# Expert chunks of five row tiles in place of two, four and four, in a two-FFN macaron kernel

## The chip, the cores and the metric

The kernel runs on one core of one Trainium2 chip. The metric is device time in microseconds (us), lower is better. The engines are called as the profile calls them: PE is the matrix engine, PEld its weight loads, DVE the vector engine, ACT the scalar engine, POOL the GpSimd engine, SP the engine that issues plain DMAs.

## The reference

A macaron block on x of 4 x 2048 rows by 256: half a mixture-of-experts FFN, an attention step, half the same FFN again. Each FFN routes every row to two of eight experts; an expert takes at most 1280 rows (1.25 x 8192 / 8), highest weights first.

```python
x = x + 0.5 * ffn(layernorm(x))
x = x + attn(layernorm(x))
x = x + 0.5 * ffn(layernorm(x))

def ffn(x):                     # D = 256, F = 1024, E = 8, two experts per row
    probs = softmax(x @ router_w.T); topw, topi = top_k(probs, 2)
    ...                         # the first 1280 rows of each expert, by weight
    g = disp @ wg; u = disp @ wu               # 1280 x 256 by 256 x 1024, each expert
    eo = (silu(g) * u) @ wd                    # 1280 x 1024 by 1024 x 256
    out[rows] += eo * weight
```

All products are in fp32.

## The kernel before

Five stages follow each other: a first router, FFN one, attention (which ends with the logits of the second router), a second router, FFN two. Both FFNs are the function `experts`; only the rows' source and the target of its sums differ. The change lies in `experts` and in the class `RowList`, which it uses.

**An expert in chunks.** An expert's 1280 rows are ten tiles of 128 rows. `SIZES` cuts them into chunks of two, four and four tiles (`chunks`, lines 414 to 416), so that an FFN has 24 chunks. For each chunk the kernel gathers the rows by index (`gather`, one indirect DMA from POOL's queue for each tile), zeroes rows that the expert doesn't own (`blank`, on ACT), transposes them on PE (`turn`, one call for each half of D; `tr` is one PSUM bank, and ACT copies it to `xsT`), makes the hidden activations (`small_steps` or `large_steps`), and multiplies by wd (the down projection, lines 656 to 683): eight matmuls for each tile, an ACT scaling into `eo`, an indirect DMA from POOL that adds the rows to the target, and then `behind(k, i)`, which hangs other work behind tile `i`.

**The small chunk.** Two tiles are 256 columns. `small_steps` makes gate and up products plainly: over four steps `p`, 2 halves of F x 2 (gate, up) x 2 halves of D, 32 matmuls of 256 columns.

**The large chunk.** Four tiles are 512 columns. `large_steps` splits D, F and the columns in halves and uses the seven-product scheme of Strassen and Winograd: in each of four steps `p`, seven products for gate and seven for up, of BH = 256 columns each, so 56 matmuls in place of 64. Its operands are sums of weights (`ws`, made by `sums_of_w` on DVE once for each expert) and sums of inputs (`xs`, `sums_of_x`, once for each large chunk). The first product goes to the bank `one`, which ACT copies to `p1`; the others go to `mm`, three buffers of two banks. One buffer holds two products for gate and up, four matmuls in all. DVE reads them in adds of 1024 elements (512 where only one product is concerned) into `ct` and `uu`; ACT applies silu in place (L536), and DVE multiplies the halves into `h` (L451, through `finish`).

**The down projection's first two tiles** are ordered so that the products with the last step's `h` come last: twelve matmuls stand between the last up product and the first use of it.

**Row lists.** `RowList` turns slots into the list of an expert's row numbers: `high` makes three vectors of 1024 elements on DVE, `low(g)` a mask of 128 x 1024 for each of eight groups (L366, int16 operands and an fp16 result; the innermost axis of the mask is the slot, along which the row's own slot is a broadcast with step 0), `products(g)` eight small matmuls, `sum` and `end` bring the result back as indices. For expert 0 of an FFN nothing can start before its list is there (lines 632 to 640). For the next expert the masks are spread over `beside` (during the steps of the small chunk) and `behind` (during the down projections of the first two chunks), and the list ends in the second chunk.

**Order.** Inside `with tc.manual_schedule` (line 643) PE, DVE and ACT run in program order, so `beside(k, p)`, called after each step, and `behind(k, i)`, called after each tile of the down projection, set where the other work falls. POOL is ordered by the framework's scheduler, and so is everything on all engines for the first list of an FFN, which stands ahead of line 643.

Of the kernel before, what the change touches and what calls it, by code (L numbers as in the profile page):

```python
# [18 lines left out]
P = 128  # L19
# [7 lines left out]
def macaron_kernel(  # L27
# [31 lines left out]
    CH = 4  # L59
# [14 lines left out]
    JL = NJ // 4  # L74
    GT = T // (P // E)
# [28 lines left out]
    nc.gpsimd.iota(count, pattern=[[1, P]], base=0, channel_multiplier=0)  # L104

# [230 lines left out]
    TG = 8  # L336
    Q = P // 32
    HI = 32 // 2

    class RowList:  # L340
# [4 lines left out]
        def __init__(self, e, pool, ppool):  # L345
            self.e, self.pool, self.ppool = e, pool, ppool
            self.lo = {}

        def high(self):
            hi = self.pool.tile([P, T, HI], F16, tag="hi", name="hi", bufs=2)  # L350
            self.hv = self.pool.tile([P, T, 2, HI], F16, tag="hv", name="hv", bufs=2)
            shape = [P, T, HI]
            nc.vector.tensor_tensor(
                hi, spread(count[:, :HI].unsqueeze(1), shape),
                spread(slot_hi[:, self.e, :].unsqueeze(2), shape), ALU.is_equal,
            )
            nc.vector.tensor_scalar(self.hv[:, :, 0, :], hi, row_in, None, ALU.mult)
            nc.vector.tensor_tensor(self.hv[:, :, 1, :], hi, spread(row_of.unsqueeze(2), shape), ALU.mult)

        def begin(self):  # L360
            self.ps = self.ppool.tile([P, P], F32, tag="one", name="ix", bufs=1)

        def low(self, g):
            lo = self.pool.tile([P, TG, P], F16, tag="lo", name="lo", bufs=6)
            shape = [P, TG, P]
            nc.vector.tensor_tensor(  # L366
                lo, spread(count.unsqueeze(1), shape),
                spread(slot_lo[:, self.e, g * TG : (g + 1) * TG].unsqueeze(2), shape), ALU.is_equal,
            )
            self.lo[g] = lo  # L370

        def products(self, g):
            lo = self.lo.pop(g)
            for t in range(g * TG, (g + 1) * TG):
                q = slice(t % Q * 32, t % Q * 32 + 32)
                nc.tensor.matmul(  # L376
                    self.ps[q, :], self.hv[:, t, :, :].rearrange("p k i -> p (k i)"), lo[:, t % TG, :],
                    start=(t < Q), stop=(t >= T - Q),
                )
# [5 lines left out]
        def end(self):  # L385
            self.ps = self.ppool.tile([P, CH * P], F32, tag="tr", name="ixT", bufs=1)[:, :P]
# [20 lines left out]
    BH = CH * P // 2  # L407

    def experts(name, src, dst, wait_for, weights, wpool, pool, ppool):
# [3 lines left out]

        SIZES = [ST % CH] * (ST % CH > 0) + [CH] * (ST // CH)
        assert SIZES[0] < CH and len(SIZES) == 3
        chunks = [(e, sum(SIZES[:k]), n) for e in range(E) for k, n in enumerate(SIZES)]
        lists, got, xTs, ws, xs = {}, {}, {}, {}, {}
        sent = {-1: list(wait_for)}

        def gather(k):  # L420
            if k >= len(chunks):
                return
            e, i0, n = chunks[k]
            got[k] = []
            for i in range(i0, i0 + n):
                r = pool.tile([P, W], F32, tag="r", name="r", bufs=14)
                nc.gpsimd.indirect_dma_start(  # L427
                    out=r, out_offset=None, in_=src[:, :],
                    in_offset=bass.IndirectOffsetOnAxis(ap=lists[e][:, i : i + 1], axis=0),
                )  # L430
                got[k].append(r)

        def blank(k, *tiles):
            for i in tiles:
                if k < len(chunks) and i < chunks[k][2]:
                    e, r = chunks[k][0], got[k][i]
                    nc.scalar.mul(r[:, 0:D], r[:, 0:D], r[:, D + E + e : D + E + e + 1])

        def turn(k, c):
            if k >= len(chunks):  # L440
                return
            n = chunks[k][2]
            if c == 0:
                xTs[k] = pool.tile([P, DC, CH * P], F32, tag="xsT", name="xsT", bufs=2)
            ps = ppool.tile([P, CH * P], F32, tag="tr", name="tr", bufs=1)
            for i in range(n):
                nc.tensor.transpose(ps[:, i * P : (i + 1) * P], got[k][i][:, c * P : (c + 1) * P], ident)  # L447
            nc.scalar.copy(xTs[k][:, c, : n * P], ps[:, : n * P])  # L448
# [17 lines left out]
        def sums_of_x(k):  # L466
            if k >= len(chunks):
                return
            v = xTs[k]
            o = xs[k] = pool.tile([P, 4, BH], F32, tag="xs", name="xs", bufs=2)  # L470
# [6 lines left out]
        def banks():  # L477
            return ppool.tile([P, 2, CH * P], F32, tag="mm", name="mm", bufs=3)

        def small_steps(k):  # L480

            e, i0, n = chunks[k]
            xT, hs = xTs.pop(k), []
            for p in range(NF):
                ps = banks()
                for j in range(2):
                    fs = slice(p * P + j * FH, (p + 1) * P + j * FH)
                    for m in range(2):
                        for c in range(DC):
                            nc.tensor.matmul(  # L490
                                ps[:, j, m * BH : (m + 1) * BH], weights[e][m][:, c, fs], xT[:, c, :BH],
                                start=(c == 0), stop=(c == DC - 1),
                            )
                g = pool.tile([P, 2, BH], F32, tag="sg", name="sg", bufs=2)
                nc.scalar.activation(g, ps[:, :, :BH], AF.Silu)  # L495
                h = pool.tile([P, 2, CH * P], F32, tag="h", name="h", bufs=NF + 2)
                tt(h[:, :, :BH], g, ps[:, :, BH:], ALU.mult)
                hs.append(h)
                yield hs

        def large_steps(k):
            e, i0, n = chunks[k]
            xT, x4, hs = xTs.pop(k), xs.pop(k), []
            late = []

            def product(ps, p, j, c, b):

                for m in range(2):
                    if c is None:
                        a = ws[e][:, m, j, p * P : (p + 1) * P]  # L510
                    else:
                        a = weights[e][m][:, c, j * FH + p * P : j * FH + (p + 1) * P]
                    nc.tensor.matmul(ps[:, m * BH : (m + 1) * BH], a, b, start=True, stop=True)  # L513

            def finish(h, ct, qs):
                tt(h[:, qs, :], ct[:, qs, 0, :], ct[:, qs, 1, :], ALU.mult)
# [3 lines left out]
            def first_product(p):  # L520
                one = ppool.tile([P, CH * P], F32, tag="one", name="one", bufs=1)
                product(one, p, 0, 0, xT[:, 0, :BH])
                p1[p] = pool.tile([P, CH * P], F32, tag="p1", name="p1", bufs=2)
                nc.scalar.copy(p1[p], one)  # L524

            first_product(0)
            for p in range(NF):
                last = p == NF - 1

                ct = pool.tile([P, 5, 2, BH], F32, tag="ct", name="ct", bufs=2)  # L530
                blocks = ct.rearrange("p q m s -> p q (m s)")
                h = pool.tile([P, 2, CH * P], F32, tag="h", name="h", bufs=NF + 2)
# [4 lines left out]

                a = banks()
                product(a[:, 0, :], p, 0, 1, xT[:, 1, :BH])
                product(a[:, 1, :], p, 1, None, x4[:, 1, :])  # L540
                tt(blocks[:, 0:5:4, :], spread(p1.pop(p).unsqueeze(1), [P, 2, CH * P]), a, ALU.add)
                if late and not last:
                    finish(*late.pop())
                b = banks()
                product(b[:, 0, :], p, 0, None, x4[:, 0, :])
                product(b[:, 1, :], p, 2, None, x4[:, 2, :])
                uu = pool.tile([P, 2, CH * P], F32, tag="uu", name="uu", bufs=2)
                tt(uu, spread(blocks[:, 4:5, :], [P, 2, CH * P]), b, ALU.add)
                tt(blocks[:, 3, :], uu[:, 1, :], b[:, 0, :], ALU.add)
                if not last:  # L550
                    first_product(p + 1)
                d = banks()
                if not last:
                    product(d[:, 0, :], p, 3, None, xT[:, 1, BH:])
                    product(d[:, 1, :], p, 1, 1, x4[:, 3, :])
                    tt(blocks[:, 1:3, :], uu, d, ALU.add)
                    silu(slice(0, 4))
                    late.append((hq, ct, slice(0, 4)))
                else:

                    silu(slice(0, 4, 3))
                    product(d[:, 0, :], p, 1, 1, x4[:, 3, :])
                    tt(blocks[:, 2, :], uu[:, 1, :], d[:, 0, :], ALU.add)
                    silu(slice(2, 3))
                    finish(*late.pop())
                    d = banks()
                    product(d[:, 0, :], p, 3, None, xT[:, 1, BH:])
                    finish(hq, ct, slice(0, 4, 2))
                    tt(blocks[:, 1, :], uu[:, 0, :], d[:, 0, :], ALU.add)
                    silu(slice(1, 2))  # L570
                    finish(hq, ct, slice(1, 4, 2))
# [3 lines left out]
        EARLY = 5  # L575
# [579 lines left out]
```

## Time and profile before

| | |
|---|---|
| runs shown, us | 2085.96, 2082.26, 2086.65 (median 2085.96) |
| profiled execution, us | 2080.76 |
| its span, first to last instruction, us | 2078.9 |
| mean granted PE clock in it | 0.952 of full speed |
| FFN one: first matmul of the steps to last down matmul, us from the start | 126.69 to 935.70 |
| attention, first DMA, and second router's end | 940.29; 1238.18 |
| FFN two: first matmul of the steps to last down matmul | 1260.44 to 2069.19 |

The profile has one record for each instruction: the engine, the line, the operation, the tile written and the tiles read without buffer numbers, the shape. Start and duration are in us; in the table of groups the mean is in ns. A bracket behind a line gives the idle time ahead of the instruction and what ended it. An fp32 matmul leaves two records (the 160 row tiles of both FFNs have 8 down matmuls each, and line 663 has 2560 records), a transpose on PE leaves one.

### The profile page before, as it was taken

Reading aid. Unit: us, or ns where it says so; the run is one execution under the profiler, and the core shown is the slowest. Engines: PE = TensorE matmul, PEld = TensorE weight load, DVE = VectorE, ACT = ScalarE, POOL = GpSimd, SP = SyncE. Lnnn points to the kernel's source line nnn. Section 1 sums busy time; section 2 is a strip of 40 time slices with the busy share of each in tenths; the row PEclk is TensorE's granted clock in tenths of the full one; section 3 lists DMA queues with packets and bytes.
Section 4 is the critical chain, followed back from the end, with each engine's and each line's share of the span. In section 5 each row is a group of like instructions: output and inputs, shape, how many; then the busy total and the mean of one; then the engine's idle time right before and its main releaser. Section 6 shows DMA issues by size and latency. Waiting matters only on the chain.

```text
span 2078.9 us, 26374 instructions
## 1 busy us (share of the span) xinstructions
PE 1898.0 (91%) x10186; PEld 1635.5 (79%) x10186; DVE 1393.2 (67%) x2303; ACT 627.6 (30%) x1233; POOL 601.2 (29%) x640
## 2 busy tenths in 40 slices
PE   6369999999999999996999618999999999999998
PEld 4258888888888888885888416888888888888886
DVE  8867676767676767455789886767675766667554
ACT  5312222222222222224556402222222222323221
POOL 5323131313131313124556302313131314040411
PEclk8579999999999999998999858999999999999999
DMA  9911213122222211115012531222121313131201
GB/s 345 293 32 38 76 38 76 38 76 45 69 69 45 79 36 38 16 16 167 21 41 84 184 127 33 56 58 78 36 78 36 81 33 83 31 89 25 48 8 18
DMA packets 99916, 147.73 MB, mean 71 GB/s; under 512 B 7496, under 2 KB 86352, under 8 KB 99664
## 3 DMA queue, kind: packets, MB, share of 16 engines
q1 hardware_dynamic: 69056, 102.77, 14.5%
q0 software_dynamic: 30720, 43.27, 12.5%
q8 instruction: 81, 1.33, 0.3%
q14 instruction: 43, 0.35, 0.1%
q10 hardware_dynamic: 16, 0.01, 0.0%
HBM read 98.84 MB, written 55.57 MB: 74 GB/s over the span
## 4 chain that ended last, share of the span: by engine, by line
PE 82%; DVE 8%; issue 1%; POOL 1%; ACT 1%; DMA 1%; POOLq 0%; DVEq 0%; SPq 0%
PE mm L513 31%; PE mm L663 27%; PE mm L490 11%; PE one L513 5%; PE pc L842 2%; PE qp L785 2%; PE tr L447 2%; PE py L900 1%; DVE above L291 1%; DVE uu L451 1%; DVE lo L366 1%; PE ix L376 1%; DVE ct L451 1%; DVE q L796 0%; DVE st L912 0%
## 5 line engine op out<-in xcount | busy, mean ns | idle before, releaser
L663 PE MATMUL mm<-wdt,h 128*128 128x256 f32 x2560 | 572.6, 381 | 3.3 <-DVE ct L451 3.3
L663 PEld LDWEIGHTS mm<-wdt,h 128*128 128x128 f32 x2560 | 478.3, 190 | 75.0 <-PE tr L447 7.5
L513 PE MATMUL mm<-xs,ws 128*128 128x256 f32 x1536 | 352.4, 379 | 0.0
L513 PEld LDWEIGHTS mm<-xs,ws 128*128 128x128 f32 x1536 | 291.8, 190 | 39.7
L671 POOL DMA_INDIRECT out_dram<-eo,ixs x80 | 129.4, 1618 | 582.4 <-ACT eo L670 441.4
L671 POOL DMA_INDIRECT acc<-eo,ixs x80 | 129.5, 1619 | 581.7 <-ACT eo L670 438.9
L451 DVE TENSOR_TENSOR ct<-p,mm 128x1024 f32<-128x1024 f32 x128 | 156.3, 1221 | 165.9 <-PE mm L513 165.9
L451 DVE TENSOR_TENSOR ct<-uu,mm 128x512 f32<-128x512 f32 (+1 forms) x288 | 245.8, 863 | 27.7 <-PE mm L513 20.8
L536 ACT ACTIVATE ct<-ct 128x1024 f32<-128x1024 f32 (+1 forms) x192 | 145.3, 772 | 377.8 <-DVE ct L451 377.8
L427 POOL DMA_INDIRECT r<-rows,ixs x160 | 164.8, 1030 | 156.0 <-issue 81.3
L451 DVE TENSOR_TENSOR h<-sg,mm 128x512 f32<-128x512 f32 x64 | 43.9, 687 | 237.3 <-ACT sg L495 237.3
L670 ACT ACTIVATE eo<-mm,r 128x256 f32<-128x256 f32 x160 | 75.9, 474 | 400.4 <-PE mm L663 400.4
L451 DVE TENSOR_TENSOR uu<-ct,mm 128x1024 f32<-128x1024 f32 x128 | 155.7, 1217 | 27.5 <-PE mm L513 27.4
L451 DVE TENSOR_TENSOR h<-ct 128x1024 f32<-128x1024 f32 (+1 forms) x160 | 158.3, 1005 | 15.4 <-ACT ct L536 15.4
L366 DVE TENSOR_TENSOR lo<-count,slot_lo 128x1024 f16<-128x1024 int16 x128 | 150.5, 1218 | 0.0
L524 ACT COPY p<-one 128x512 f32<-128x512 f32 x128 | 75.0, 586 | 239.6 <-PE one L513 239.6
L490 PE MATMUL mm<-xsT,wgt 128*128 128x256 f32 x512 | 133.2, 383 | 0.0
L490 PE MATMUL mm<-xsT,wut 128*128 128x256 f32 x512 | 132.7, 382 | 0.0
L513 PE MATMUL mm<-xsT,ws 128*128 128x256 f32 x512 | 131.4, 379 | 0.0
L490 PEld LDWEIGHTS mm<-xsT,wut 128*128 128x128 f32 x512 | 98.4, 192 | 13.7
L513 PEld LDWEIGHTS mm<-xsT,ws 128*128 128x128 f32 x512 | 97.3, 190 | 13.2
L490 PEld LDWEIGHTS mm<-xsT,wgt 128*128 128x128 f32 x512 | 96.8, 192 | 12.9 <-ACT xsT L448 0.7
(205 smaller groups left out, 2538.6 us busy)
## 6 DMA issues: line engine op xcount, KB each, us to landing
wgt<-in_L_ffn_wg_dram SPq DMA_DIRECT2D x16, 1024.0 KB, 4.9
wut<-in_L_ffn_wu_dram SPq DMA_DIRECT2D x16, 1024.0 KB, 7.2
wdt<-in_L_ffn_wd_dram SPq DMA_DIRECT2D x16, 1024.0 KB, 5.3
rows<-xw SPq DMA_DIRECT2D x7, 2176.0 KB, 11.0
xw<-in_L_attn_x_dram SPq DMA_DIRECT2D x16, 512.0 KB, 8.9
xw<-acc SPq DMA_DIRECT2D x16, 512.0 KB, 8.8
out_dram<-xw SPq DMA_DIRECT2D x16, 512.0 KB, 2.9
r<-rows,ixs POOLq DMA_INDIRECT x160, 2.8
```

The costliest lines, as they stand in the source:

```text
L366: nc.vector.tensor_tensor(lo, spread(count.unsqueeze(1), shape), spread(slot_lo[:, self.e, g * TG : (g + 1) * TG].unsqueeze(2), shape), AL ...
L427: nc.gpsimd.indirect_dma_start(out=r, out_offset=None, in_=src[:, :], in_offset=bass.IndirectOffsetOnAxis(ap=lists[e][:, i : i + 1], axis=0),)
L447: nc.tensor.transpose(ps[:, i * P : (i + 1) * P], got[k][i][:, c * P : (c + 1) * P], ident)
L451: nc.vector.tensor_tensor(o, a, b, op)
L490: nc.tensor.matmul(ps[:, j, m * BH : (m + 1) * BH], weights[e][m][:, c, fs], xT[:, c, :BH], start=(c == 0), stop=(c == DC - 1),)
L513: nc.tensor.matmul(ps[:, m * BH : (m + 1) * BH], a, b, start=True, stop=True)
L524: nc.scalar.copy(p1[p], one)
L536: nc.scalar.activation(ct[:, qs, 0, :], ct[:, qs, 0, :], AF.Silu)
L663: nc.tensor.matmul(po[i], hs[p][:, j, i * P : (i + 1) * P], weights[e][2][:, j * NF + p, :], start=(p == 0 and j == 0), stop=(p == NF - 1 ...
L670: nc.scalar.mul(eo, po[i], got[k][i][:, D + e : D + e + 1])
L671: ins = nc.gpsimd.indirect_dma_start(out=dst[:, :], out_offset=bass.IndirectOffsetOnAxis(ap=lists[e][:, i0 + i : i0 + i + 1], axis=0), in_ ...
L785: nc.tensor.matmul(qp[i][:, k, 0:W1], xT[i][:, k, c, :], wqx[:, c, :], start=(c == 0), stop=(c == DC - 1))
```

## The change

- Chunks: every expert now has two chunks of five tiles (640 columns), all with the seven-product scheme at BH = 320. `small_steps` is gone. Five tiles are gathered, blanked and transposed for each chunk; a turn takes three or two tiles of one half of D (`TURN`), so a chunk has four turns in place of two.
- PSUM: a buffer of `mm` now holds one product for gate and up, each in a bank of its own (320 of 512 columns are used); `one` holds a single matmul, so the first product is made and copied in two parts, `m = 0` and `m = 1`, at different places of the step before.
- DVE: seven adds of 640 elements in each step. `finish` moves to POOL in the first three steps of a chunk, and stays on DVE in the last step.
- `ct` loses its fifth block; `u2`, `xs`, `hi`, `hv` have one buffer, `h` has four (before: six), `lo` five (before: six).
- The list of the next expert is made wholly in the down projection of the first chunk (`behind`, step 0), and nothing of it stands beside the steps. `sums_of_w` and the last gather of an expert go to the down projection of the second chunk.
- The first list of an FFN (`waited_for`) has masks with the tile innermost: `counts`, a constant of 128 x 128 x 8 int16, is compared with eight slots, and PE reads `lo` and `hv` with strides.
- The start of an FFN is now inside the manual order: list, gathers of two chunks, sums of weights, then blanks and turns of three tiles. The first three products of step 0 need only these; the other two tiles, the second half of the turns and `sums_of_x` follow them (`rest_of_first`). In this chunk every second blank is on DVE.

The core of the diff:

```diff
-    CH = 4
+    CH = 5
+    BANK = 512
...
+    counts = const.tile([P, P, TG], I16, name="counts")
+    nc.gpsimd.iota(counts, pattern=[[1, P], [0, TG]], base=0, channel_multiplier=0)
...
         def low(self, g):
+            lo = self.pool.tile([P, TG * P], F16, tag="lo", name="lo", bufs=5)
+            at = slot_lo[:, self.e, g * TG : (g + 1) * TG]
+            if self.waited_for:
+                lo = lo.rearrange("p (s t) -> p s t", t=TG)
+                nc.vector.tensor_tensor(lo, counts, spread(at.unsqueeze(1), [P, P, TG]), ALU.is_equal)
+                self.lo[g] = lo.rearrange("p s t -> p t s")
+            else:
...
         def turn(k, q):
+            c, i0, i1 = q // 2, (0, TURN)[q % 2], (TURN, CH)[q % 2]
+            ps = ppool.tile([P, BANK], F32, tag="tr", name="tr", bufs=1)
+            for i in range(i0, i1):
+                nc.tensor.transpose(
+                    ps[:, (i - i0) * P : (i - i0 + 1) * P], got[k][i][:, c * P : (c + 1) * P], ident
+                )
+            nc.scalar.copy(turned[k][:, c, i0 * P : i1 * P], ps[:, : (i1 - i0) * P])
...
+        def rest_of_first():
+            blank(0, *range(TURN, CH))
+            for q in (1, 3):
+                turn(0, q)
+            sums_of_x(0)
...
+            def both(p, *what):
+                ps = banks()
+                for m in range(2):
+                    product(p, m, ps[:, m, :BH], *what)
+                return ps[:, :, :BH]
...
+            first_product(0, 0)
+            for p in range(NF):
+                last = p == NF - 1
...
+                p2 = both(p, 0, 1, xT[:, 1, :BH])
+                if p == 0:
+                    first_product(0, 1)
+                    if k == 0:
+                        rest_of_first()
+                    x4 = xs.pop(k)
+                tt(ct[:, 0], p1[p], p2, ALU.add)
+                if last:
+                    silu(slice(0, 1))
+                tt(u2, p1.pop(p), both(p, 1, None, x4[:, 1, :]), ALU.add)
+                tt(ct[:, 3], u2, both(p, 2, None, x4[:, 2, :]), ALU.add)
+                first_product(p + 1, 0)
+                tt(ct[:, 2], ct[:, 3], both(p, 1, 1, x4[:, 3, :]), ALU.add)
+                if last:
+                    silu(slice(2, 3))
+                p5 = both(p, 0, None, x4[:, 0, :])
+                tt(ct[:, 1], u2, p5, ALU.add)
+                tt(ct[:, 3], ct[:, 3], p5, ALU.add)
+                first_product(p + 1, 1)
+                if last:
+                    silu(slice(3, 4))
+                    finish(nc.vector, slice(0, 4, 2))
+                tt(ct[:, 1], ct[:, 1], both(p, 3, None, xT[:, 1, BH:]), ALU.add)
+                if last:
+                    silu(slice(1, 2))
+                    finish(nc.vector, slice(1, 4, 2))
+                else:
+                    silu(slice(0, 4))
+                    finish(nc.gpsimd, slice(0, 4))
...
         def beside(k, p):
+            if p == 1:
+                blank(k + 1, 0, 1, 2)
             elif p == 2:
+                blank(k + 1, 3, 4)
+            if p > 1:
+                turn(k + 1, p - 2)

         def behind(k, i):
+            if step == 0 and more:
                 if i == 0:
+                    more = following[0] = RowList(e + 1, pool, ppool)
+                    more.high()
+                    for g in range(3):
                         more.low(g)
+                    more.begin()
+                elif i == 1:
+                    more.products(0)
+                    for g in (3, 4, 5):
+                        more.low(g)
+                elif i == 2:
+                    for g in (1, 2, 3):
+                        more.products(g)
+                    for g in (6, 7):
+                        more.low(g)
+                elif i == 3:
+                    for g in (4, 5):
+                        more.products(g)
+                elif i == 3.5:
+                    for g in (6, 7):
+                        more.products(g)
+                    more.sum()
+                elif i == 4:
+                    lists[e + 1] = more.end()
+                    gather(k + 2)
             elif step == 1:
+                if i in (1, 2):
+                    sums_of_w(e + 1, i - 1)
+                elif i == 3:
+                    gather(k + 2)
+            if i in (0, 1):
+                turn(k + 1, 2 + i)
+            elif i == 2:
+                sums_of_x(k + 1)
...
+        with tc.manual_schedule(engines=ENGINES - {mybir.EngineType.Pool}):
+            first.high()
+            first.begin()
+            for g in range(NL):
+                first.low(g)
+                first.products(g)
+            first.sum()
+            lists[0] = first.end()
+            gather(0)
+            gather(1)
             for m in range(2):
                 sums_of_w(0, m)
+            blank(0, *range(TURN))
+            for q in (0, 2):
+                turn(0, q)
```

## The prediction

> **What bounds the kernel now.** I read the page's busy times first, then the granted clock and busy times by stretch, then PE's waits, then the timeline of one step and of an FFN's start.
>
> The stretches (length, then busy us and records of PE, PEld, DVE, ACT, POOL, then PE clock, DMA share, GB/s):
>
> ```profile
> core 0: us, PE busy (x) PEld busy (x) DVE busy (x) ACT busy (x) POOL busy (x), PEclk, DMA share, GB/s
> 400.00:500.00 100.00, 99.82 (x529) 86.86 (x528) 66.19 (x77) 27.54 (x51) 25.86 (x20) 1.00 0.25 58
> 1500.00:1600.00 100.00, 99.82 (x530) 86.84 (x529) 65.45 (x78) 27.56 (x51) 25.83 (x20) 1.00 0.25 59
> ```
>
> Both FFNs, 1618 of 2079 us, are PE at full clock with 0.2% idle; DVE is the next engine, at 66%. So FFN time is PE work, and the change is worth what PE work it takes away, unless it brings stalls. A busy PE need not be PE at its peak, so the rate is read from starts:
>
> ```profile
> 322.81 7.93 PE L663 MATMUL mm<-wdt,h 128*128 128x256 f32 x36
> 330.58 1.03 PE L490 MATMUL mm<-xsT,wgt 128*128 128x256 f32 x4
> ...
> 340.94 0.60 PE L447 MATMUL tr<-ident,r 128*128 128x128 f32 x4
> 341.38 1.03 PE L490 MATMUL mm<-xsT,wgt 128*128 128x256 f32 x4
> ```
>
> 36 records take 330.58 - 322.81 = 7.77 us: 0.2158 us for a record of 256 columns, so 0.4317 for an fp32 matmul. Transposes of 128 columns take 0.44 / 4 = 0.110. The two give 0.83 ns a column, nearly proportional.
>
> The groups with their mean in ns, which price everything below:
>
> ```profile
> L451 DVE TENSOR_TENSOR ct<-p,mm 128x1024 f32<-128x1024 f32 x128 | 156.3, 1221 | 165.9 <-PE mm L513 165.9
> L366 DVE TENSOR_TENSOR lo<-count,slot_lo 128x1024 f16<-128x1024 int16 x128 | 150.5, 1218 | 0.0
> L451 DVE TENSOR_TENSOR ct<-uu,mm 128x512 f32<-128x512 f32 x192 | 128.7, 684 | 4.4
> L536 ACT ACTIVATE ct<-ct 128x1024 f32<-128x1024 f32 x96 | 101.4, 1056 | 228.4 <-DVE ct L451 228.4
> L524 ACT COPY p<-one 128x512 f32<-128x512 f32 x128 | 75.0, 586 | 239.6 <-PE one L513 239.6
> L802 POOL TENSOR_TENSOR q<-q,m 128x512 f32<-128x512 f32 x32 | 33.9, 1059 | 12.2 <-DVE m L801 11.5 <-PE py L900 0.4
> ```
>
> FFN one's start, where PE isn't the bound:
>
> ```profile
> 104.62 1.22 DVE L353 TENSOR_TENSOR hi<-count,slot_hi 128x1024 f16<-128x1024 int16 x1 [0.19 <-issue]
> ...
> 108.43 8.02 DVE L366 TENSOR_TENSOR lo<-count,slot_lo 128x1024 f16<-128x1024 int16 x7
> ...
> 118.71 0.17 DVE L391 CAST ixs<-ixf 128x16 int32<-128x16 f32 x1
> ...
> 123.08 0.51 ACT L437 ACTIVATE r<-r 128x256 f32<-128x256 f32 x1 [5.74 <-DMA r<-rows,ixs]
> ...
> 126.69 1.92 PE L490 MATMUL mm<-xsT,wgt 128*128 128x256 f32 x4
> ...
> 130.04 1.03 PE L490 MATMUL mm<-xsT,wgt 128*128 128x256 f32 x4
> ```
>
> The reader sees masks on DVE back to back, the index ready at 118.88, the first tile 4.2 us later, and matmuls from 126.69 at half speed until 130.0.
>
> **What the skill says.** "TensorE: Matmul & The Clock Gate", Back-to-back issue gap, gives N/2.4 + 2.5 ns warm; with two passes for a record, (2 x 256)/2.4 + 2.5 = 215.8 ns, which the trace matches, and (2 x 320)/2.4 + 2.5 = 269.2 for the new size, an estimate. The same page, Part 1, has the clock at half speed until some 3.4 us of activity; the trace has 0.50 from 126 to 130 us and 1.00 after. "VectorE: DVE Perf Modes", perf-mode tier table, gives a 16-bit tensor_tensor twice the rate if all steps are one. Today's masks run at one element a cycle (1218 ns for 1024; their slot operand has step 0); no two-input operation of before shows the fast mode. "SBUF — State Buffer", Door 1, says that reads which hit a new 16-byte line each time pay a penalty; PE's reads of the new `lo` step 16 bytes. No run shows the price.
>
> **The change part by part.**
>
> *Steps, PE.* Before, an expert makes 32 + 2 x 56 = 144 matmuls of 256 columns: 144 x 0.4317 = 62.16 us. After, 2 x 56 = 112 of 320: 2 x 0.2692 = 0.538 each by the formula, 0.5396 in proportion; 60.3 to 60.4. I take 1.8 us an expert, 16 experts: **-28.4 us** (27.6 to 30). Down matmuls (80), transposes (20) and list products (64) of an expert are the same in number. PE's weight loads (190 ns) stay shorter than a record (269).
>
> *Steps, can DVE keep up?* One add of 640: from 684 at 512 and 1221 at 1024, 1.05 ns an element, 818 ns. Seven make 5.7 us; a step's 14 matmuls take 7.54. Played through with 0.2 us from a matmul's end to DVE's start, the adds begin at 1.28, 2.36, 3.43, 5.05, 6.13, 6.95 and 7.75 us of the step, and the tightest buffer of `mm`, p5's, which two adds read, is free at 7.77 while its next user starts at 8.63. So 0.86 us are to spare; no stall. `one`: the copy of 320 columns is some 0.43 us on ACT (586 at 512); its next user comes 2.2 us later.
>
> *POOL's finish.* 1059 ns at 512 scales to 2.65 us for 1280 (from 2.1 ns an element). The one that can be late is step 2's: silu (1.27 us from 1056) ends some 2.4 us into step 3, POOL at 5.1; step 3 has only 12 matmuls, 6.5 us, and the down projection reads that `h` after four more, at 8.2. To spare: 3.1 us. Step 0's finish stands behind five gathers (1.25 us apart) which wait for the list, but it is ready only 9 us into the chunk. In step 3 the last product ends at 6.5; the queue on DVE (fifth and sixth add, finish, last add), silu and finish end at 10.3, and PE wants them after 12 down matmuls at 11.7.
>
> *List and sums beside the down projection.* It lasts 40 x 0.4317 = 17.3 us plus turns and list products, 19.5. DVE has `high` 2.8, eight masks at 1.13 (8.02 for seven) 9.1 and `sums_of_x` 1.7, after 3.8 us of the last step: done at 17.4. Masks are ready before their products (mask 3 at 10.2, wanted at 11.7). In the second chunk `sums_of_w` (8 x 0.62) and `sums_of_x` end near 12. Turn 3 follows turn 2 through the one bank `tr`, with 0.86 us of matmuls between; eo and the copy on ACT just fit. I allow **+1 us** in all for such edges; before has the like:
>
> ```profile
> PE mm L663 <- DVE ct L451: 3.3, 16, 0.4
> ```
>
> *FFN starts (two).* List: ten masks and vectors, each 0.61 us apart if the fast mode comes (1.13 before), so the last mask is done at 111.1 in place of 116.45. From there to the index 2.43 us, less 0.6 because a sum of weights no longer slips between reduce and cast; 0.5 more for PE's strides: index at 113.5, **5.4 us earlier**. After it three tiles are needed, not two: third gather lands near +7.1, blank to 7.6, transposes and two copies through `tr` to 9.5, three products' four matmuls at half clock (1.08 each) to 13.9, then ACT frees itself for the fifth blank at 14.5, turns 1 and 3 with copies to 17.0, second sum at 17.6. Only then does PE go on, idle for 3 us of this. Counting done work (4 x 0.54, six more transposes 0.65) at full clock, the stream starts at +14.8 if PE stays at full speed, +16.5 if it must warm again: 128.3 to 130.0. Before, by the same count (8 records done at 130.04), 128.3. Cost 0 to 1.7 us each; I take 1: **+2 us**.
>
> *No cost:* the larger iota (POOL makes it in the first microseconds; its first use is at 104), the tail (last matmul to end, 2078.9 - 2069.2 = 9.7 us, the same scatters).
>
> **Sum.** -28.4 + 1 + 2 = -25.4 us. On the profiled execution's own time, 2080.76 (span 2078.9 and 1.9 around it), 2055.4; the median shown, 2085.96, lies 5.2 above it. I forecast from the median: **2060 us**.
>
> **Rivals.**
> (B) The first lists stay slow: fast mode not taken, or PE's strided reads as long as the masks. Then the index comes only 0.6 earlier, at 118.2, and a start costs 118.2 + 15.6 - 128.3 = 5.5 us: -28.4 + 1 + 2 x 5.5 = -16.4: 2070. For: no trace line shows the mode. Against: all operands are 16-bit with step one.
> (C) A small wait returns in every chunk, at tile 0 and 1 (turn 3 behind turn 2, banks of `mm` changing use) or at step 3's end: 0.4 us x 32 = 12.8 on the full sum: 2073. For: three chains of step 3 have slacks of about a microsecond. Against: before passes the same places with 0.2 us.
> (D) Slower: POOL becomes the bound. The place is the fifth down matmul, which waits for step 2's `h`. The price is finish's length beyond its 3.1 us of slack, in all 32 chunks; from 25.4 / 32 = 0.8 us of stall, a finish of 6.6 us, or one queued behind a scatter or gather that waits, the gain is gone. At 8 us: 2 x 32 = 64 less 25, 2121 at a median of 2086. For: POOL's order is the scheduler's, and its pace at 1280 elements isn't in the trace. Against: POOL is 26% busy in the FFNs, and DVE's adds read one operand from PSUM.
>
> **Numbers.** Forecast 0.67, B 0.14, C 0.13, D 0.06. The forecast's own range is 2052 to 2067 (28 to 30 of work, starts 0 to 1.7, the runs' spread of 4 us); with B and C the range is 2051 to 2074. A measurement of this kernel can tell about 0.2%, 4 us, from no change. D holds nearly all that is slower; a mixture of B and C reaches "same". Faster 0.93, same 0.02, slower 0.05.
>
> **What would show it.** Right: 112 matmuls of 320 columns an expert, two records of 0.269 us each, PE at 99.8% in stretches like those above, no wait of PE on POOL, DVE near 70%; the span of FFN one, first to last matmul, some 13 us shorter. Masks of the first lists near 0.69 us, small products still 0.4 a group. Wrong: waits of `mm` on DVE or POOL with counts of 16 or 32; `h` on POOL over 5 us; records of 320 columns at more than 0.28; a list that ends later than 9 us after `slot_lo`.

## The result, and the profile after

| | before | after |
|---|---|---|
| median of four runs, us | 2085.09 (2082.26 to 2086.65) | 2051.34 (2050.27 to 2051.76) |
| ratio, 95% interval | | 0.9839 [0.9822, 0.9856] |
| profiled execution, us (span) | 2080.76 (2078.9) | 2051.27 (2049.4) |
| end of `slot_lo` to last down matmul, FFN one, us | 104.44 to 935.70 = 831.26 | 104.23 to 920.28 = 816.05 |
| the same, FFN two, us | 1238.18 to 2069.19 = 831.01 | 1222.19 to 2039.60 = 817.41 |
| end of `slot_lo` to the first index, us (both FFNs) | 14.44, 14.46 | 8.93, 8.93 |
| last down matmul of FFN one to second `slot_lo`, us | 302.48 | 301.91 |

The kernel is 33.75 us faster by the medians and 29.5 by the two profiled spans: 15.2 in FFN one, 13.6 in FFN two, the rest in code that didn't change. Before's profiled execution is not one of its four; after's is.

The page's busy times, and then a stretch of steady work (columns as before):

```profile
PE 1879.1 (92%) x9162; PEld 1439.7 (70%) x9162; DVE 1413.5 (69%) x2499; ACT 656.8 (32%) x1357; POOL 882.3 (43%) x737
```

```profile
core 0: us, PE busy (x) PEld busy (x) DVE busy (x) ACT busy (x) POOL busy (x), PEclk, DMA share, GB/s
400.00:500.00 100.00, 100.00 (x474) 75.82 (x473) 69.07 (x90) 29.48 (x59) 44.70 (x27) 1.00 0.26 59
```

PE stays the bound, and the last 0.18 us of idle in 100 are gone. POOL's share has gone from 26 to 45, which nobody waits for yet. The rate of PE from its starts, one step and one expert (PE's timeline of after, then of before):

```profile
336.45 0.70 PE L529 MATMUL mm<-xsT,wgt 128*128 128x320 f32 x2
...
343.98 0.70 PE L529 MATMUL mm<-xsT,wgt 128*128 128x320 f32 x2
...
378.44 0.27 PE L410 MATMUL ixT<-ident,sums 128*128 128x128 f32 x1
...
477.71 0.27 PE L410 MATMUL ixT<-ident,sums 128*128 128x128 f32 x1
```

```profile
392.76 0.27 PE L387 MATMUL ixT<-ident,sums 128*128 128x128 f32 x1
...
493.90 0.27 PE L387 MATMUL ixT<-ident,sums 128*128 128x128 f32 x1
```

A step's 28 records take 7.53 us, 0.2691 each. An expert, from the transposed list to the next one, takes 99.27 us; in the trace of before the same two points lie 101.14 apart. The gain is 1.87 us for each of 16 experts, 29.9 in all. The columns of an expert's steps have gone from 144 x 256 = 36864 to 112 x 320 = 35840: what is saved is an eighth of the products of the two tiles that were multiplied plainly.

The groups that the prediction priced (table of groups, mean in ns):

```profile
L482 DVE TENSOR_TENSOR ct<-ct,mm 128x640 f32<-128x640 f32 x384 | 313.0, 818 | 104.2 <-PE mm L529 95.5 <-PE one L529 2.1 <-issue 0.8
L561 POOL TENSOR_TENSOR h<-ct 128x1280 f32<-128x1280 f32 x96 | 279.0, 2906 | 424.7 <-ACT ct L558 421.5 <-ACT r L465 2.9
```

The adds have the length predicted, POOL's multiply is a tenth longer. PE's waits in the steps, where before had 16 waits on DVE in the down projection, 3.3 us in all:

```profile
PE mm L529 <- DVE xs L482: 2.0, 2, 1.0
PE mm L529 <- DVE ct L482: 0.2, 1, 0.2
```

And FFN one's start:

```profile
106.15 4.90 DVE L386 TENSOR_TENSOR lo<-counts,slot_lo 128x1024 f16<-128x1024 int16 x8
...
112.99 0.17 DVE L414 CAST ixs<-ixf 128x16 int32<-128x16 f32 x1
...
122.55 1.27 PE L529 MATMUL one<-xsT,wgt 128*128 128x320 f32 x2
...
126.61 0.42 ACT L546 COPY p<-one 128x320 f32<-128x320 f32 x1 [2.33 <-PE one L529]
126.94 0.51 ACT L465 ACTIVATE r<-r 128x256 f32<-128x256 f32 x1
...
129.71 3.94 PE L529 MATMUL mm<-xs,ws 128*128 128x320 f32 x8 [0.99 <-DVE xs L482]
133.49 0.70 PE L529 MATMUL one<-xsT,wgt 128*128 128x320 f32 x2
```

Eight masks take 4.90 us, 0.61 apart, and the index is ready 5.7 us earlier than before. The fifth tile's blank on ACT comes behind the copy of the second first product, whose matmul ends only then; the transposes of the fifth tile, the sums and eight matmuls follow. Those eight last 3.94 us, much longer than the 2.32 that eight take in a step: the granted clock, full from 126.0 us on, is at half again from 129.4 to 132.8.

### The profile page after: what moved, and what is told of

Same layout as the page of the kernel before. It is cut to its first block, busy times and chain, and to the rows that moved or that the text cites. A ratio compares the mean times of both kernels' runs of the same rounds, so it can differ in the third digit from the quotient of the medians.

```text
span 2049.4 us, 24693 instructions
## 1 busy us (share of the span) xinstructions
PE 1879.1 (92%) x9162; PEld 1439.7 (70%) x9162; DVE 1413.5 (69%) x2499; ACT 656.8 (32%) x1357; POOL 882.3 (43%) x737
## 4 chain that ended last, share of the span: by engine, by line
PE 83%; DVE 6%; POOL 2%; issue 1%; ACT 1%; DMA 1%; POOLq 0%; DVEq 0%; ACTq 0%; SPq 0%
PE mm L529 41%; PE mm L675 27%; PE one L529 7%; PE tr L476 2%; PE pc L856 2%; PE qp L799 2%; PE ix L399 1%; PE py L914 1%; DVE above L298 1%; DVE q L810 1%; DVE st L926 0%; DVE xw L924 0%; DVE cand L305 0%; DVE m L815 0%; PE trx L791 0%
## 5 line engine op out<-in xcount | busy, mean ns | idle before, releaser
L561 POOL TENSOR_TENSOR h<-ct 128x1280 f32<-128x1280 f32 x96 | 279.0, 2906 | 424.7 <-ACT ct L558 421.5
L529 PE MATMUL mm<-xs,ws 128*128 128x320 f32 x1536 | 459.1, 435 | 2.2 <-DVE xs L482 2.0
L482 DVE TENSOR_TENSOR ct<-ct,mm 128x640 f32<-128x640 f32 x384 | 313.0, 818 | 104.2 <-PE mm L529 95.5
L558 ACT ACTIVATE ct<-ct 128x320 f32<-128x320 f32 (+1 forms) x224 | 181.8, 813 | 284.5 <-DVE ct L482 284.5
L482 DVE TENSOR_TENSOR ct<-p,mm 128x640 f32<-128x640 f32 x128 | 105.0, 821 | 238.5 <-ACT p L546 200.4
L482 DVE TENSOR_TENSOR ct<-u,mm 128x640 f32<-128x640 f32 x256 | 210.1, 821 | 59.7 <-PE mm L529 55.8
L546 ACT COPY p<-one 128x320 f32<-128x320 f32 x256 | 108.5, 424 | 406.4 <-PE one L529 404.2
L685 POOL DMA_INDIRECT acc<-eo,ixs x80 | 132.8, 1661 | 221.1 <-ACT eo L684 214.1
L529 PE MATMUL mm<-xsT,ws 128*128 128x320 f32 x512 | 158.7, 432 | 0.0
L482 DVE TENSOR_TENSOR u<-p,mm 128x640 f32<-128x640 f32 x128 | 104.9, 820 | 15.6 <-PE mm L529 12.5
L529 PE MATMUL one<-xsT,wgt 128*128 128x320 f32 x256 | 91.3, 439 | 0.0
## 6 DMA issues: line engine op xcount, KB each, us to landing
rows<-xw SPq DMA_DIRECT2D x7, 2176.0 KB, 10.6
```

Of the source, the lines that this page charges most:

```text
L482: nc.vector.tensor_tensor(o, a, b, op)
L529: nc.tensor.matmul(ps, a, b, start=True, stop=True)
L546: nc.scalar.copy(p1[p][:, m, :], one[:, :BH])
L558: nc.scalar.activation(ct[:, qs, 0, :], ct[:, qs, 0, :], AF.Silu)
L561: engine.tensor_tensor(hq[:, qs, :], ct[:, qs, 0, :], ct[:, qs, 1, :], ALU.mult)
L685: ins = nc.gpsimd.indirect_dma_start(out=dst[:, :], out_offset=bass.IndirectOffsetOnAxis(ap=lists[e][:, i0 + i : i0 + i + 1], axis=0), in_ ...
```

## The experiments

The runs were made on three chips, on which before has medians of 2080.16 to 2080.85, some 4 to 5 us less than above. So ratios to before are compared, or times within one chip.

### Two parts by themselves: chunks of five, fast first lists

After once more; after with the first lists' masks laid out as they were; and before with only its first lists made fast.

```diff
# slow_first_lists (from after)
-        following = [RowList(0, pool, ppool, waited_for=True)]
+        following = [RowList(0, pool, ppool)]
# before_fast_lists (from before): counts and waited_for as in the change, and
-        following = [RowList(0, pool, ppool)]
+        following = [RowList(0, pool, ppool, waited_for=True)]
```

> The changed kernel itself, run beside the others so that all are timed against the same runs of the kernel before. Main theory (the gain is fewer PE columns, 1.87 us for each expert in the trace, and starts that cost about as much as the fast lists give): 2051 +- 2 us, span near 2049. What it also tells: whether the profiled execution of the kernel before (2080.76) was a low one of its kind. If the spread of before is that of its single executions, its median here is 2083 to 2087 and the ratio 0.983 to 0.985; if the execution with a profile is the true one, before comes out near 2081 and the ratio is 0.986.

> The changed kernel with the first list of each FFN made as all other lists are (slot innermost[...]). Main theory (the fast masks end ten vector operations 0.53 us earlier each, nothing else moves): both FFN starts 5.3 us later, 10.6 us in all, 2062; the index comes 8.9 to 9.1 us after the list's first operation in place of some 8.6 less 5.3; steady stretches unchanged. Rival (PE's strided reads or the clock at the start eat part of it): 4 to 8 us. Rival (the lists carry the whole gain of the change): 2075 or more.

> The kernel before with nothing but the fast first lists of the change. Main theory: 5.3 us for each FFN, 10 to 11 us in all, 2074 to 2075 at a median of 2085 before; then chunks of five are worth the rest of the change, some 23 us, in which each start costs about 6 us more (three tiles, seven-product operands) and the steady part gives 30. Rival (the lists only help a start that has five tiles): 0 to 3 us.

| one chip, us | lists as before | fast lists |
|---|---|---|
| chunks of two, four, four | 2080.74 | 2071.28 (ratio 0.9958 [0.9943, 0.9973]) |
| chunks of five | 2059.23 (0.9896 [0.988, 0.9911]) | 2047.79 (0.9845 [0.983, 0.986]) |

`after_again` (bottom right) is 3 us faster than expected, and before, at 2080.74, does not show here the higher times of the result. The parts nearly add up: chunks of five bring 21.5 us, fast lists 9.5 (10 to 11 expected), both 33.0; with chunks of five the lists bring 11.4 (10.6 expected). In the traces with chunks of five the first index comes 14.1 us after `slot_lo` with the old lists and 8.9 with fast ones. And chunks of five alone bring 8 us less than their 29.9 of steady work. The two starts lose it: in the trace of `slow_first_lists` each FFN takes 807.4 us from the first index to the last down matmul, 9.3 less than before, where the steps of eight experts are 15.0 shorter. The lists give it back.

### What the start costs

Two other orders of an FFN's first chunk. In `start_woven` ACT blanks the fifth tile before it copies the first product, and the other tiles' transposes stand between the first products; in `all_tiles_first` everything is ready before the first product.

```diff
# start_woven
+            if k == 0:
+                blank(0, *range(TURN, CH))
             first_product(0, 0)
+            if k == 0:
+                turn(0, 1)
...
-                p2 = both(p, 0, 1, xT[:, 1, :BH])
+                p2 = both(p, 0, 1, xT[:, 1, :BH], between=(lambda: turn(0, 3)) if k == p == 0 else None)
...
-                        rest_of_first()
+                        sums_of_x(0)
```

> The changed kernel with the FFN's start woven: ACT blanks the fifth tile before it copies the first product, the turn of tiles four and five for the first half of D stands behind the first product, that for the second half between gate and up of the second, so sums of x are ready when PE wants them. Main theory (at an FFN's start PE waits some 3 us because ACT, in program order, blanks the fifth tile only after it has copied the last of the first products, and then PE runs at half clock for another 3.7 us): PE has no gap over 0.7 us after its first product, full clock stays from then on, 4 to 5 us for each FFN, 8 to 10 in all, 2042. Rival (the tile's gather lands too late, so order on ACT is nothing): 0 to 2 us. Rival (the clock falls again anyway): 4 to 6 us in all.

```diff
# all_tiles_first
                 turn(0, q)
+            rest_of_first()
...
-                    if k == 0:
-                        rest_of_first()
```

> After with the whole of rest_of_first (blanks of tiles 4 and 5, turns 1 and 3, sums_of_x) ahead of the first product, as an FFN's start would be without the three-tile trick. Theory 1 (in after the fifth blank stands on ACT behind the copy of the first product, so that PE's early products only delay the other tiles and are themselves made at half clock): 2 to 5 us faster than after, so 2043 to 2046 beside the 2047.8 that after had. Theory 2 (the three early products are real gain, because they hide the fourth and fifth tile's landing): 3 to 6 us slower, 2051 to 2054.

`start_woven`: 2040.76 us, ratio 0.981 [0.9796, 0.9823], 7.0 us below after on the same chip (8 to 10 expected) and the fastest kernel here. `all_tiles_first`: 2046.51, ratio 0.9836 [0.982, 0.9852], which can't be told from after's 0.9845. PE's timeline of `start_woven`, then of `all_tiles_first`, then of `after_again` at both starts:

```profile
127.56 2.32 PE L522 MATMUL mm<-xs,ws 128*128 128x320 f32 x8
129.72 0.70 PE L522 MATMUL one<-xsT,wgt 128*128 128x320 f32 x2
```

```profile
129.76 2.37 PE L529 MATMUL mm<-xs,ws 128*128 128x320 f32 x8
131.96 0.70 PE L529 MATMUL one<-xsT,wgt 128*128 128x320 f32 x2
```

```profile
129.56 3.90 PE L529 MATMUL mm<-xs,ws 128*128 128x320 f32 x8 [0.99 <-DVE xs L482]
133.30 0.70 PE L529 MATMUL one<-xsT,wgt 128*128 128x320 f32 x2
...
1246.45 2.42 PE L529 MATMUL mm<-xs,ws 128*128 128x320 f32 x8 [0.99 <-DVE xs L482]
1248.71 0.70 PE L529 MATMUL one<-xsT,wgt 128*128 128x320 f32 x2
```

The reader sees one program with two starts: with the same gaps ahead of them, the eight products take 3.90 us in FFN one and 2.42 in FFN two. The granted clock (PEclk) tells them apart. Four stretches of `after_again`, the first two from FFN one's start, the others from FFN two's:

```profile
core 0: us, PE busy (x) PEld busy (x) DVE busy (x) ACT busy (x) POOL busy (x), PEclk, DMA share, GB/s
125.77:129.18 3.41, 1.53 (x7) 0.62 (x5) 0.66 (x2) 1.58 (x4) 1.03 (x2) 1.00 0.34 92
129.18:132.60 3.42, 3.04 (x6) 2.06 (x7) 2.36 (x5) 0.00 (x0) 0.00 (x0) 0.50 0.02 5
1241.93:1245.34 3.41, 2.13 (x9) 1.12 (x8) 0.33 (x1) 1.21 (x3) 2.15 (x3) 1.00 0.35 106
1245.34:1248.76 3.42, 2.43 (x11) 1.67 (x10) 2.92 (x6) 0.37 (x1) 0.00 (x0) 1.00 0.15 41
```

"TensorE: Matmul & The Clock Gate", Part 1, says that the gate watches windows of some 3.4 us that run freely, so that the same kernel can warm up at different points. The traces agree: in all twelve, the stretches of one granted clock last 3.41 us or a multiple of it, but for those that the ends of a trace cut. FFN one's first full window falls on the gaps, with PE busy for 1.53 us, and the next one is at half clock; FFN two's holds more of the early products, 2.13 us, and the clock stays.

From the first index to the last down matmul the six FFN executions of this start (after, `after_again` and `lows_beside_steps` below) take 804.5 to 808.5 us, mean 806.4: 806.7 to 808.5 in the four in which the clock fell back, 804.5 and 804.7 in the other two. `all_tiles_first` takes 804.9 and 804.4, `start_woven` 802.4 and 802.3: without the gaps the clock does not fall back, in any of the four. So `all_tiles_first` is as good as a start of after that keeps the clock, and weaving brings some 2 us more.

So the three-tile start is no gain: its early products run while the clock is low, put ACT's copy ahead of the fifth blank, and leave a gap that may cost the clock. The gain expected of all tiles first is at the edge of what these runs can tell; in the traces it is the half-clock start that doesn't come.

### POOL's multiply: its slack

The multiply of gate and up on DVE, one step late; and on POOL, made twice or three times over.

```diff
# finish_on_dve
+                if late:
+                    hq_, ct_ = late.pop()
+                    tt(hq_, ct_[:, :, 0, :], ct_[:, :, 1, :], ALU.mult)
                 tt(ct[:, 3], u2, both(p, 2, None, x4[:, 2, :]), ALU.add)
...
-                    finish(nc.gpsimd, slice(0, 4))
+                    late.append((hq, ct))
# pool_finish_x2, pool_finish_x3: range(2), range(3)
-                    finish(nc.gpsimd, slice(0, 4))
+                    for _ in range(2):
+                        finish(nc.gpsimd, slice(0, 4))
```

> The changed kernel with the multiply of silu and up on DVE in the first three steps too, one step late, ahead of the third add of the next step. Main theory (PE sets the pace as long as DVE's work in a step is under PE's): DVE has 7 x 0.82 + 1.49 = 7.2 us of 7.54 in a step; played through, the third add starts at 4.6 us where PE wants its buffer at 6.5, so 0 to 3 us slower in all, DVE near 85% busy in the steady stretches. Rival (DVE at 95% of a step becomes the bound, each queue gap counts): 0.3 us or more for each of 96 steps, 30 us slower. Rival (POOL's multiply costs something today[...]): faster by 3 us or more.

> The changed kernel with POOL's multiply done twice (same output). Main theory (it has 3 us of slack): 2 x 2.9 = 5.8 us end 0.5 to 1.0 us before the fifth down matmul wants step 2's h: within 2 us of the changed kernel. Rival (POOL's multiply is near the path already, or holds gathers and scatters back): 20 us or more slower.

> The changed kernel with POOL's multiply done three times (same output). Main theory: 8.7 us a step is more than a step's 7.54, so the third one ends some 26 us after the first could begin at 9.2, at about 35.3 us of a chunk, where PE wants it at 31.0: 4 to 5 us for each of 32 chunks, 130 to 160 us slower, all in the wait of the down projection on POOL. Rival (the scatters and gathers behind it also come late and hold PE in the next chunk): 200 us or more.

Measured on one chip: 2059.46 (ratio 0.9898 [0.9869, 0.9926]), 2066.11 and 2335.17, the last two in one run each, against after's 2047.79 at the same level of before (2080.74 there, 2080.85 here). All three are slower than their main expectations. `finish_on_dve` (11.7 us slower) lies between 0 to 3 and its rival's 30, `pool_finish_x2` (18) near its rival's 20, `pool_finish_x3` (287) beyond its rival's 200. `finish_on_dve`, a stretch and the wait that answers to it:

```profile
400.00:500.00 100.00, 99.66 (x472) 75.44 (x471) 76.22 (x96) 29.78 (x60) 28.07 (x20) 1.00 0.25 59
```

```profile
PE ix L399 <- DVE lo L390: 4.7, 14, 0.3
```

The late multiply pushes DVE's last step, and with it the masks of the next list, back: one wait in each of 14 lists, and an expert that takes 99.81 us in place of 99.27 (from one of these waits, at 168.18 us, to the next; 0.34 of the 0.54 is the wait itself). That is 2 x 7 x 0.54 = 7.6 us of the 11.7. Both its starts ran their eight products at half clock (20.4 us from the index to the second step, as in after's FFN one), where one of `after_again`'s two did, which by the times above is worth some 2 us; the rest stays open.

`pool_finish_x2`, waits of PE and the timeline of one last step:

```profile
PE ix L399 <- DVE lo L390: 10.1, 14, 0.7
...
PE mm L529 <- DVE ct L482: 6.8, 14, 0.5
```

```profile
353.76 5.89 POOL L561 TENSOR_TENSOR h<-ct 128x1280 f32<-128x1280 f32 x2 [1.73 <-ACT ct L558]
...
358.65 1.68 DVE L561 TENSOR_TENSOR h<-ct 128x640 f32<-128x640 f32 x1
```

No PE waits on POOL here. What is late is DVE's own first half of `h`, whose operands are both in SBUF: it takes 1.68 us in place of 0.82, and ends 0.7 us after POOL does. It needs 0.7 us from POOL's end, hardly less than its usual 0.82, and so seems to do its work only when POOL's is done. The two waits shown make 16.9 of the 18.3 us. With three multiplies both ends are hit, and the mean granted clock is 0.92, in place of 0.955 in `after_again`:

```profile
PE mm L676 <- POOL h L561: 95.5, 32, 3.2
PE mm L529 <- DVE ct L482: 85.6, 50, 3.5
```

### List masks beside the steps

The change has all masks in the down projection. Here `high` and three `low` of the next list go behind the four steps of the first chunk; then the three `low` alone.

```diff
         def beside(k, p):
+            e = chunks[k][0]
+            if k % PER == 0 and e + 1 < E:
+                if p == 0:
+                    following[0] = RowList(e + 1, pool, ppool)
+                    following[0].high()              # not in lows_beside_steps
+                else:
+                    following[0].low(p - 1)
...
                 if i == 0:
-                    more = following[0] = RowList(e + 1, pool, ppool)
-                    more.high()                      # stays in lows_beside_steps
-                    for g in range(3):
-                        more.low(g)
                     more.begin()
```

> The changed kernel with the next list begun beside the steps of the first chunk, as the kernel before had it beside its small chunk: the three vectors of the list's high part behind step 0, one mask behind each of steps 1 to 3, the other five masks in the down projection. Main theory: DVE has 1.8 us free in a step, but the buffers of mm leave only about 1 us of delay at a step's first add; the high part (2.8 us) holds PE up by 0.9 to 1.2 us once in each of 14 chunks, a mask (1.2 us) not at all: 13 to 17 us slower, the waits of mm on DVE counted 14 to 28. Rival (a vector operation with two operands in memory and POOL's multiply, 2.9 us, exclude one another): 2 to 3 us for each of the four places, 100 us or more. Rival (DVE at 69% has room): nothing.

> After with three low masks of the next list behind steps 1, 2 and 3 of an expert's first chunk, high left in the down projection. Theory 1 (of the masks moved in masks_beside_steps only the multiply of high with two operands in memory cost time, because it ran beside POOL's multiply): no change, within 3 us of after. Theory 2 (any 1.2 us of masks in a step makes DVE late): 3 of 6.5 us of the masks moved, so about half of the 89.6 us: 30 to 50 us slower.

`masks_beside_steps`: 2137.43, ratio 1.0272 [1.0242, 1.0302], about 90 us slower than after and slower than before, where 13 to 17 us were expected. `lows_beside_steps`: 2046.21, ratio 0.9843 [0.9827, 0.986], no difference from after. So three masks of 1.22 us cost nothing in a step, and `high` nearly all: the rival of the exclusion is right, in one place of the four. The timeline of `masks_beside_steps` behind the first step, and PE's wait:

```profile
350.90 2.95 POOL L561 TENSOR_TENSOR h<-ct 128x1280 f32<-128x1280 f32 x1 [8.59 <-ACT ct L558]
351.02 3.91 DVE L376 TENSOR_TENSOR hv<-hi,row_of 128x1024 f16<-128x1024 f16 x1
...
355.72 1.44 PE L529 MATMUL mm<-xs,wgt 128*128 128x320 f32 x2 [3.35 <-DVE ct L482]
...
356.95 1.27 PE L529 MATMUL mm<-xs,wut 128*128 128x320 f32 x2
...
361.21 1.52 PE L529 MATMUL mm<-xsT,ws 128*128 128x320 f32 x4
362.57 0.70 PE L529 MATMUL mm<-xsT,wgt 128*128 128x320 f32 x2
```

```profile
PE mm L529 <- DVE ct L482: 47.0, 14, 3.4
```

And a mask in `lows_beside_steps`:

```profile
349.57 1.22 DVE L390 TENSOR_TENSOR lo<-count,slot_lo 128x1024 f16<-128x1024 int16 x1
...
351.09 2.91 POOL L561 TENSOR_TENSOR h<-ct 128x1280 f32<-128x1280 f32 x1 [4.62 <-ACT ct L558]
```

The last vector of `high` starts 0.12 us after POOL's multiply and takes 3.91 us where it has 1.22 in after; it ends 1.1 us after POOL does, so most of its own work fell there. The mask of 1.22 us in the other kernel is over before POOL starts. "SBUF — State Buffer", Who interferes with whom, says that a DVE instruction with two inputs in SBUF contends with a GpSimd instruction that reads SBUF, and that the one that starts first keeps the shared ports to its end. The lines agree in both kernels, here by 2.7 us of 3.91; DVE's adds, with one operand in PSUM, keep their 0.82 us beside POOL (0.823 at most, in all of the 305 here that overlap its multiply).

PE pays twice: it waits 3.35 us, and then runs at half clock until 361.8, so that 14 records take 6.85 us (355.72 to 362.57), where 3.77 are due. 3.35 + 3.08 is 6.43 us, and 14 places make the 90.

## Why the prediction was right, and what was off in size

The forecast was 2060 with 2051 to 2074 around it; the run gave 2051.34, at the very edge, and below the 2052 to 2067 of the forecast alone. The mechanism was right: PE at full clock with less to multiply, and no new stall in the steps. That the number lies inside the range is luck, by 0.34 us. From the median of 2085.96 the sum was -25.4; measured are -33.75 by the medians.

- **Steps, PE: right, and rounded too low.** The record of 320 columns was to be 0.2692 us and is 0.2691. By that figure the step was 62.16 - 60.30 = 1.86 us an expert; I took 1.8 between two ways of scaling, and 1.87 came. The proportional scaling, 60.4, was the wrong one.
- **Edges, +1: came to nothing.** All that isn't steps takes 38.93 us of an expert, by the starts of PE's records, where before has 38.96: the idle 0.18 us went, but list products and down matmuls take 0.38 more, and the transposes with that idle time 0.41 less. With the steps: -29.9, where -27.4 stood.
- **FFN starts, +2: the mis-sized term.** Its first half held: masks 0.61 apart, index 5.5 us earlier after `slot_lo` (5.4 predicted, and 113.16 for 113.5). PE's strided reads, put at 0.5 us for each list, cost 0.3: from the last mask to the copy of the sums it is 0.92 us, 0.63 in `slow_first_lists`. A group of eight small products lasts 0.72 us, though, not 0.4. The sums were to be there 17.6 us after the index; PE's first product of them starts at 16.55. What I had as one number has two values, with the clock or without: over six FFNs the time from index to last down matmul is 806.4 on average, 10.3 us below the 816.7 of before's two. With the list's 5.5 that is 15.8 for each FFN, of which 15.0 (eight experts of 1.87) are steady work: the start brings 0.8 each, where I had it cost 1. In the profiled execution alone it is 0.2 in FFN one and a loss of 1.4 in FFN two (whose clock was at half until 1245.6 us and again from 1249.0 to 1252.4), nearer to the prediction.
- **DVE, POOL.** An add of 640 is 818 ns, as predicted; DVE has 69%, predicted near 70. POOL's finish is 2.91 us for 2.65. No PE wait on POOL was right, but its reason was incomplete: the slack does not end at the fifth down matmul, 3.1 us on, but where DVE's two-operand multiply starts. A POOL multiply of 5.89 us, hardly over the 5.75 (2.65 and 3.1 of slack) that I had called free, already costs 18 us.
- **The down projection's list** fits, as played through; PE's only new wait in the steps is 0.2 us, once. FFN one from first to last matmul became 11.3 us shorter (809.0 to 797.7); I had said some 13.

For the two traced executions the sum closes: steps and edges -29.9, starts +1.1, code that is the same -0.7, in all -29.5 where -25.4 stood. For the medians it doesn't quite. Of the 8 us between -25.4 and -33.75 the terms above explain 2.5 (steps and edges) and, by the mean of the starts, 3.6. The rest, some 2 us, is of the size by which single executions differ in code that is the same in both kernels (from FFN one's last down matmul to the second `slot_lo`, 300.8 to 303.2 us in the executions of after and its variants). Before's slower executions left no trace, so this stays open.

On the rivals. **B** (slow lists) did not come, and `slow_first_lists` shows its price: 11.4 us, I had 9 (-16.4 for -25.4). **C** (a wait in each chunk) did not come; `finish_on_dve` shows what it looks like, 0.54 us for each list. **D** (POOL as the bound) did not come, but its place and price were both wrong: DVE is hit first, and a multiply of 8.8 us gave 2335, far above my 2121 for 8 us. That sum was also off in itself: 2086 + 64 - 25 is 2125.

## What to carry to other kernels

Where PE is the bound, count its records and price them by the rate that starts show, with its fixed part for each record, and do not average that with a rougher scaling. Before work is moved to POOL or beside it, list DVE's instructions with two SBUF operands and keep them out of POOL's time; adds that read PSUM can run beside it. At a start, order the engines that feed the last tile first, and let PE have its first products in one stretch: gaps of about a microsecond each cost their length and, depending on when they fall, the clock as well.

## What had not been expected of the hardware

- A 16-bit vector of 1024 on DVE took 3.91 us beside a POOL multiply and 1.22 otherwise, and an fp32 one of 640 1.68 in place of 0.82. Neither shows as a wait: the instruction is busy longer.
- A wait of PE of 3.35 us cost 6.4, since matmuls ran at half speed for some 6 us behind it.
- The same gaps of about 1 us in a start left the clock at full speed in one FFN and at half in the other: 2.2 us between the two starts of one execution. In the twelve traces, a window of 3.41 us at full clock in which PE was busy, by its records, for 46% or less was always followed by half clock, and one with 54% or more never.
- PE's strided reads of `lo` and `hv` have a price, but a hidden one. The 64 small products of FFN one's first list, in after and then in `slow_first_lists` (shortest, median and longest in ns), both at half clock:

```profile
L399 PE MATMUL ix<-lo,hv x64: 400/412/482, 106.9 to 111.4; 128*32 128x128 f16 x64
L399 PE MATMUL ix<-lo,hv x64: 263/300/314, 108.1 to 116.1; 128*32 128x128 f16 x64
```

They still keep pace with masks 0.61 us apart, so only the last group's delay shows.
